# Placing keys by TensorE and giving more steps a choice of engine in a gated-attention kernel

## The chip, the core and the metric

One core of a Trainium2 chip runs the whole program. The metric is the device time of one execution in microseconds (us), the median of several. A profiled execution has its own time, and the profile's span lies inside it.

## What is computed

The input x has 2 batches of 2048 rows of 512 numbers; a context has 77 rows per batch. Four steps follow one another, each added to x with a gate:

```
x = x + tanh(g_xattn[0]) * attention0(layernorm(x), ctx, mask, Wq, bq, Wk, bk, Wv, bv, Wo, bo)  # 16 heads of 32
x = x + tanh(g_ffn[0])   * int8_matmul(layernorm(x), rhs)            # rows rounded to int8 by their absmax
x = x + tanh(g_xattn[1]) * attention1(layernorm(x), ctx, Wq, Wk, Wv, Wo, bo)  # 16 heads of 64
x = x + tanh(g_ffn[1])   * prototypes(layernorm(x), ...)  # top 2 of 32 experts of rank 16
layernorm(x) = (x - mean) / sqrt(var + 1e-5)
```

All products must be nearly f32: most operands are kept as two f16 parts (high and low), and a product is made of three f16 products.

## The kernel before, in words

The 4096 rows are 32 tiles of 128 rows; up to 11 tiles are in work at once. Each tile passes through L0, F0, L1 and M1, the four steps above. Ahead of them stands the preparation, which begins with the weights' loading and overlaps the first tiles: prepK, prepQ and prepV make keys, queries' weights and values of layer 0, prepA and prepU fold layer 1's keys and values into the weights (tiles A and U), prepR rounds rhs, prepM prepares the prototypes. prep0b and prep1b make the same tables for the second batch; they go to DRAM and come back when tile 16 begins.

**Who sets the order.** Nothing is issued where it is written. Every call is recorded by the class Clock with a cost for its engine, its port and its inputs. Where a step may go on one of several engines, `first_of` records all of them (`tt`, `cpy`, `zero` use it). After recording, `refine` places all instructions forward and backward several times, choosing for each the engine that ends it first; then `kick` shifts due times at random by seeds from the list `kicks`, and an order is kept when its planned end is earlier. What comes out is one fixed list per engine. Each engine works through its list in order, so a late instruction holds back everything behind it. All DMAs are issued by SyncE (SP), in one list too.

**The filler.** `lulls` looks for planned gaps of TensorE within the first 270 us and fills them with matmuls on a constant tile, `heat`, which write to a bank that nobody reads (L1737). There are 126 of them: 44 ahead of the first projection, 82 later. They keep TensorE busy and compute nothing.

**Keys of layer 0 (build_k).** The scores of a head are one matmul over 128 rows: queries stand as high, high, low parts of 32 rows each and 32 rows of a constant; the keys (`kst`) as high, low, high parts and rows with mask and bias. ScalarE and VectorE split the keys `kf` (128 rows are 4 heads of 32) into the f16 parts in a buffer; 12 DMAs then move 32-row pieces of them to their rows in `kst`. The bias rows come from 8 matmuls per two batches with `bsel` into 4 rows, another split, and further DMAs, in the first batch over DRAM (`kb_d`).

**Values of layer 0 (build_v).** For each f16 part a zeroed buffer is filled in four 32-row pieces by ScalarE from `vf`, for the low part also by VectorE; matmuls with slices of the identity (`ipad`) then place them.

**Layer norm (ln).** VectorE takes mean and variance, GpSimd adds EPS and scales (128x1), GpSimd raises to the power -1/2, VectorE makes the negated mean term and then the normalised row in one 128x512 step. **hl_T** makes the f16 high part with a ScalarE copy (128x512), the low part with a GpSimd subtraction, and transposes both by DMA. **probs_T** does the same to probabilities of 128x1232. **F0** rounds to int8 by adding and taking away a large constant, both on ScalarE.

A line that most instructions carry in the profile, L468, is the line of the recorder; they are told apart by their tiles.

Of the kernel before, what the change touches and what calls it, by code (L numbers as in the profile page):

```python
# [21 lines left out]
P = 128  # L22
# [83 lines left out]
class Clock:  # L106
# [272 lines left out]
    def kick(self, seed, start, last):  # L379

        rng = np.random.RandomState(seed)
        width, amp = rng.choice([40.0, 120.0, 2000.0]), rng.choice([0.5, 1.5, 4.0, 10.0])
        at = rng.rand() * max(last)
        z = rng.randn(max(self.block) + 1) * amp
        return [t + z[b] if abs(s - at) < width else t for s, t, b in zip(start, last, self.block)]
# [137 lines left out]
def first_of(choices, *a):  # L523

    alts = []
    for e, op, late in choices:
        outs, ins = e.parts(a, {})
        st = e.stages(op, outs, ins)
        alts.append((st, late, lambda f=getattr(e.e, op): f(*map(real, a))))
    c = e.clock  # L530
    best = min(range(len(alts)), key=lambda i: c.probe(alts[i][0], ins, outs) + alts[i][1] * alts[i][0][0][1])
    st, late, fn = alts.pop(best)
    alts.insert(0, (st, late, fn))
    c.add(fn, st, ins, outs, choices[best][0].name, alts)
@with_exitstack
def flamingo(ctx: ExitStack, tc: tile.TileContext, I, out):
    nc = tc.nc
    opt = dict(first=(11, 10, 3, 4, 3), carve=('uuuu', 'utt'), bufs=(11, 11, 4, 5, 4, 2), pol=(22, 0, 1.0, 0, -0.5), pr=(10, 0, 5, 5, 0, 0, 0, 0), keep=5, bias=(1, 0.6, 1, 0.5), win=-1, bonus=(0, 0, 0, -2), l1=1, res=(0, 1), ref=8, heat=270.0, lat=(0.05, 0.1, 1), whole=(6, 1, 1, 0, 0))
    opt["kicks"] = (200002, 200006, 200010, 200020, 200022, 200023, 200029, 200030, 200035, 200036, 200065, 200078, 200080, 200082, 200094, 200158, 200159, 200168, 200183, 200199, 200203, 200206, 200227, 200261, 200293, 200318, 200320, 200327, 200348, 200361, 200362, 200381, 200391, 200394, 200398, 200413, 200424, 200442, 200446, 200487, 200504, 200512, 200517, 200541, 200633, 200666, 200677, 200706, 200723, 200804, 200812, 200845, 200911, 200928, 200929, 200976, 201087, 201098, 201152, 201161, 201200, 201229, 201254, 201555, 201746, 201975, 202128, 202218, 202497, 202749, 203015, 203029, 203041, 203217, 203435, 203614, 203656, 203838, 203897, 204467, 204750, 204971, 205446, 205590, 205835, 205893, 206161, 206172, 206676, 206898, 207521, 207706, 208282, 208578, 209511, 211890, 212426, 212442, 212830, 212838, 213041, 213114, 213149, 213243, 213251, 213257, 213277, 213358, 213478, 213509, 213654, 213776, 213865, 213994, 214325, 214334, 214336, 214408, 214502, 214813, 216675, 216876, 217994, 218441, 218747, 220507, 220570, 222551, 223022, 230339, 230361)
# [12 lines left out]
    def cpy(*a):  # L552
        first_of(((V, "tensor_copy", bias_[1]), (SC, "copy", 0.0)), *a)

# [83 lines left out]
    def f16v(t):  # L638
        return t.bitcast(F16)
# [192 lines left out]
    kb_d = dr.tile([2, H, S], F16, tag="kb_d", name="kb_d")  # L832
# [11 lines left out]
    sBb = ct("sBb", [P, NB])  # L844

    def build_k(b, dst):


        t = yield from acq("E")
        hl = f16v(t)[:, : 8 * S].rearrange("p (a g s) -> p a g s", a=2, g=4)  # L850
        split(hl[:, 0], hl[:, 1], kf[:, :, b * S : (b + 1) * S], sKb[:, b : b + 1])
        m = kst[96:] if b == 0 else f16v(t)[96:, 8 * S : 8 * S + FL].rearrange("p (h s) -> p h s", s=S)
        cpy(m, mk[96:, b, :].unsqueeze(1).broadcast_to([32, H, S]))
        for i, a in enumerate((0, 1, 0)):
            for j in range(4):
                d = dst[32 * i : 32 * i + 32].rearrange("p (g j) s -> p g j s", j=4)
                SY.dma_start(out=d[:, :, j, :], in_=hl[32 * j : 32 * j + 32, a])
        yield True
        yield from until("bsel", "q")
        ps2 = mm(), mm()  # L860
        bl = f16v(t)[:4, 8 * S + FL : 16 * S + FL].rearrange("p (a g s) -> p a g s", a=2, g=4)
        for g2, ps in enumerate(ps2):
            for g in range(2):
                PE.matmul(ps[:4, g * S : (g + 1) * S], bsel[:, 2 * g2 + g, :], kf[:, 2 * g2 + g, b * S : (b + 1) * S],
                          start=True, stop=True)
            gs = slice(2 * g2, 2 * g2 + 2)
            split(bl[:, 0, gs], bl[:, 1, gs], ps[:4, : 2 * S].rearrange("p (g s) -> p g s", g=2), sBb[:4, b : b + 1])
        d = (kb_d if b == 0 else dst[96:98]).rearrange("a (g j) s -> j a g s", j=4)
        for a in range(2):
            SY.dma_start(out=d[:, a], in_=bl[:, a])  # L870
        if b == 0:
            SY.dma_start(out=dst[96:98], in_=kb_d)
        else:
            SY.dma_start(out=dst[98:], in_=m[2:])
        rel("E", t)
        yield True
# [14 lines left out]
    bsel = ct("bsel", [P, 4, 4])  # L891

    def prepB():
        zero(bsel)
        for j in range(4):
            V.tensor_copy(bsel[32 * j : 32 * j + 32, :, j], bq[32 * j : 32 * j + 32, :])
        yield True
        yield from until("rowd")
        SC.activation(tg, gv, AF.Tanh)
        V.tensor_scalar(gb0, row[:, :D], tg[:, 0:1], None, ALU.mult)  # L900
        V.tensor_scalar(cf, tg[:, 2:3], 2.0 ** -11, None, ALU.mult)
        V.tensor_scalar(mk, mk, -1.0, 1.0, ALU.mult, ALU.add)
        V.tensor_scalar(mk, mk, 0.0, -1.0, ALU.is_equal, ALU.add)
        V.tensor_reduce(anyv, mk, AX.X, ALU.max)
        V.tensor_scalar(anyv, anyv, 1.0, None, ALU.add)
        for b in range(NB):
            V.tensor_scalar(mk[:, b, :], mk[:, b, :], anyv[:, b : b + 1], BIG, ALU.mult, ALU.mult)
        sw["row"] = True
        sw["bsel"] = True
        yield True  # L910

    def prepQ():
        w = yield from wget("wq0")
        yield from norm2(1, w, wq0h.rearrange("p k n -> p (k n)"))
        absmax(17, bq)
        V.tensor_tensor(mx[:, 1:2], mx[:, 1:2], mx[:, 17:18], ALU.max)
        yield True
        sWq = pow2_of("sWq", gmax("amQ", 1, 2))
        yield from until("kf")
        V.reciprocal(c0, S_["K"])  # L920
        V.tensor_scalar(c0, c0, 2.0 ** 32, None, ALU.mult)
        V.tensor_tensor(sWq, sWq, c0, ALU.min)
        V.tensor_tensor(c0, sWq, S_["K"], ALU.mult)
        V.tensor_scalar(sBb, anyv, c0, 1.0 / (512.0 * BIG), ALU.mult, ALU.mult)
        V.reciprocal(c0, c0)
        V.tensor_scalar(c0, c0, 512.0 * 32.0 ** -0.5, None, ALU.mult)
        sw["c0"] = True
        split(wq0h, wq0l, w, sWq)
        yield True
        wrel("wq0")  # L930
        sw["q"] = True


    def build_v(b, v0):
        for hl in range(2):
# [3 lines left out]
            for j in range(4):  # L939
                r = slice(32 * j, 32 * j + 32)  # L940
                c = slice(128 + j * S, 128 + (j + 1) * S)
                src = vf[r, :, b * S : (b + 1) * S]
                SC.activation(vbd[r, :, c], src, AF.Copy, scale=S_["V"][r, :])
                if hl:
                    V.scalar_tensor_tensor(vbd[r, :, c], src, S_["V"][r, :], vbd[r, :, c],
                                           ALU.mult, ALU.subtract)
            yield True
            for half in range(2):
                ps = mm()
                for q in range(5):  # L950
                    k = half * 5 + q
                    h0, h1 = blk_heads(k)
                    o = ps[:, q * 96 : q * 96 + 96]
                    gs = sorted({h // 4 for h in range(h0, h1)})
                    for i, g in enumerate(gs):
                        w0 = 128 + 128 * k - 308 * g
                        st = 96 - 32 * (4 * g - h0)
                        PE.matmul(o, vbd[:, g, w0 : w0 + 128], ipad[:, st : st + 96],
                                  start=(i == 0), stop=(i == len(gs) - 1))
                cpy(v0[:, hl, half * 5 : half * 5 + 5, :],  # L960
                        ps[:, :480].rearrange("p (q n) -> p q n", n=96))
                yield True
            rel("E", vs)

# [22 lines left out]
    def prep0b():  # L987

        yield from build_k(1, kst1_d)
# [285 lines left out]
    def ln(c):  # L1275
# [7 lines left out]
        G.tensor_scalar(rr, mv[:, 1:2], EPS, 2.0 ** -22, ALU.add, ALU.mult)  # L1283
# [4 lines left out]
        V.scalar_tensor_tensor(xn, xt, rr, m.broadcast_to([P, D]), ALU.mult, ALU.add)  # L1288
# [3 lines left out]
    def hl_T(xn):  # L1292
        hl = yield from acq("u")
        h = f16v(hl)
        SC.copy(h[:, :D], xn)
# [10 lines left out]
    def probs_T(E, pack):  # L1306
# [3 lines left out]
        SC.copy(ph[:, :FL], E)  # L1310
# [116 lines left out]
    def F0(c):  # L1427
# [8 lines left out]
        SC.activation(xn, xn, AF.Identity, bias=magic, scale=iv)  # L1436
# [3 lines left out]
        SC.activation(h, xn, AF.Identity, bias=unmagic)  # L1440
# [344 lines left out]
```

## Time and profile before

| What | Value |
|---|---|
| Median of 3 runs | 978.26 us (977.76 to 978.44) |
| Profiled execution: time, span | 980.5 us, 978.7 us |
| Busy: PE (TensorE) | 940.9 us, 96%, 6306 instructions |
| Busy: ACT (ScalarE) | 756.6 us, 77% |
| Busy: DVE (VectorE) | 749.2 us, 77% |
| Busy: POOL (GpSimd) | 644.8 us, 66% |
| Chain that ended last, by engine | PE 60%, DVE 16%, DMA 7%, ACT 7%, POOL 5%, issue 3% |

PE is TensorE's matmuls, PEld its weight loads. A busy PE need not be PE at its peak, because matmuls are pipelined and overlap their records: a 512-column matmul has a record of 379 ns, but the next one starts about 215 ns later. An f32 matmul leaves two records. A group's row names line, engine, operation, output<-input, the shape and the count; behind the bar stand the engine's idle time just before it, and what ended that.

### The profile page before, as it was taken

How to read it: one execution, taken by the hardware profiler on the slowest of the kernel's cores; microseconds unless marked ns; L12 is line 12 of the kernel's file. 1: busy time of each engine (PE TensorE's matmuls, PEld its weight loads, DVE VectorE, ACT ScalarE, POOL GpSimd, SP SyncE). 2: the span in 40 equal slices, each digit the busy share in tenths (PEclk: the TensorE clock that was granted, in tenths of full speed). 3: DMA queues.
4: the chain of work that ended last, by engine and by line, in shares of the span. 5: the costliest groups of instructions: out<-in, count | busy, mean ns of one | idle time of the engine just before them, and what ended most of it. 6: DMA issues, size and time to landing. Idle time of an engine off the chain costs nothing.

```text
span 978.7 us, 20530 instructions
## 1 busy us (share of the span) xinstructions
PE 940.9 (96%) x6306; PEld 512.8 (52%) x6306; DVE 749.2 (77%) x2153; ACT 756.6 (77%) x2669; POOL 644.8 (66%) x808
## 2 busy tenths in 40 slices
PE   9987889999999999999999999999999999999998
PEld 6865444555555555555455544545554555445543
DVE  3898879888978876886896788679787877865574
ACT  2878979998878798676899689677985899637521
POOL 2346568988668377667676966777668667654652
PEclk9998999999999999999999999999999999999999
DMA  9589996569999989999887899988479767753354
GB/s 318 189 216 199 165 210 132 116 137 175 200 192 187 186 164 189 180 155 192 169 166 153 152 229 204 186 147 156 83 160 191 154 109 159 124 102 71 71 113 124
DMA packets 491423, 159.67 MB, mean 163 GB/s; under 512 B 472113, under 2 KB 472625, under 8 KB 491185
## 3 DMA queue, kind: packets, MB, share of 16 engines
q1 hardware_dynamic: 491313, 158.37, 81.2%
q8 instruction: 49, 0.80, 0.3%
q14 instruction: 61, 0.50, 0.2%
HBM read 32.58 MB, written 14.35 MB: 48 GB/s over the span
## 4 chain that ended last, share of the span: by engine, by line
PE 60%; DVE 16%; DMA 7%; ACT 7%; POOL 5%; issue 3%; SPq 0%; DVEq 0%; POOLq 0%; ACTq 0%
PE bank L468 58%; DVE bank L468 5%; ACT E L468 5%; DVE s_x L468 4%; DVE u L468 2%; PE bank L1737 2%; DMA u<-W 2%; DVE x L468 2%; POOL u L468 1%; DMA u<-u 1%; POOL pp L468 1%; DMA v<-u 1%; POOL s_x L468 1%; POOL E L468 1%; ACT u L468 1%
## 5 line engine op out<-in xcount | busy, mean ns | idle before, releaser
L468 ACT ACTIVATE E<-bank,s_x,c 128x77 f32<-128x77 f32 x1024 | 412.9, 432 | 44.3 <-DVE s_x L468 39.0
L468 PEld LDWEIGHTS <-u 128*128 128x128 f16 x2324 | 198.3, 97 | 191.0 <-DMA u<-W 7.5
L468 ACT ACTIVATION_READ_ACCUMULATOR E<-bank,s_x,c 128x1 f32 x1024 | 225.7, 220 | 0.0
L468 PE MATMUL bank<-A,u 128*128 128x462 f16 (+1 forms) x864 | 190.6, 336 | 5.2 <-DVE x L468 1.7
L468 POOL TENSOR_TENSOR pp<-E,pp 128x1232 f16<-128x1232 f32 (+3 forms) x128 | 172.0, 1355 | 25.2 <-ACT pp L468 18.0
L468 PEld LDWEIGHTS <-W 128*128 128x128 f16 (+1 forms) x1540 | 119.7, 98 | 111.7 <-DMA W<-u 4.1
L468 PE MATMUL bank<-U,pt 128*128 128x512 f16 (+1 forms) x646 | 175.3, 379 | 0.0
L468 DVE TENSOR_REDUCE bank<-bank 128x6 f32<-128x462 f32 (+1 forms) x192 | 112.6, 587 | 37.2 <-PE bank L468 30.7
L468 PEld LDWEIGHTS <-pt 128*128 128x128 f16 (+1 forms) x1256 | 93.7, 98 | 84.5 <-DMA pt<-pp 8.9
L468 POOL TENSOR_SCALAR s_x<-s_x 128x1 f32<-128x1 f32 (+1 forms) x160 | 32.5, 203 | 113.4 <-DVE s_x L468 103.9
L468 DVE SCALAR_TENSOR_TENSOR x<-bank,c,x 128x512 f32<-128x512 f32 x96 | 71.1, 742 | 39.8 <-PE bank L468 39.5
L468 DVE BATCH_NORM_STATS2 s_x<-x 128x6 f32<-128x512 f32 x128 | 87.8, 686 | 7.9 <-DMA x<-x_dram 6.6
L468 ACT CAST pp<-E 128x1232 f16<-128x1232 f32 x64 | 78.3, 1226 | 17.5 <-POOL E L468 17.0
L468 POOL TENSOR_TENSOR u<-u,u 128x512 f16<-128x512 f32 x61 | 70.6, 1162 | 27.6 <-ACT u L468 26.8
L468 POOL TENSOR_TENSOR E<-E,s_x 128x1232 f32<-128x1232 f32 x32 | 71.9, 2248 | 22.9 <-DVE s_x L468 19.6
L468 PE MATMUL bank<-U,W 128*128 128x512 f16 x282 | 79.2, 379 | 0.2 <-DMA W<-pp 0.2
L468 POOL TENSOR_TENSOR s_x<-s_x,mhalf 128x1 f32<-128x1 f32 x128 | 70.0, 548 | 8.5
L468 PE MATMUL bank<-AA,u 128*128 128x512 f16 x228 | 67.0, 379 | 0.0
L468 PE MATMUL bank<-BB,u 128*128 128x512 f16 x228 | 66.5, 379 | 0.1
L468 ACT CAST u<-u 128x512 f16<-128x512 f32 x61 | 38.0, 624 | 31.3 <-DVE u L468 23.5
L468 DVE SCALAR_TENSOR_TENSOR u<-x,s_x,bank 128x512 f32<-128x512 f32 x75 | 55.4, 742 | 1.2 <-POOL W L468 0.2
L468 PE MATMUL bank<-wq0h,u 128*128 128x512 f16 x168 | 49.0, 379 | 0.8 <-ACT s_x L468 0.8
(331 smaller groups left out, 1791.5 us busy)
## 6 DMA issues: line engine op xcount, KB each, us to landing
x<-x_dram SPq DMA_DIRECT2D x32, 256.0 KB, 3.1
out_dram<-x SPq DMA_DIRECT2D x32, 256.0 KB, 2.4
A_d<-pp SPq DMA_DIRECT2D x8, 308.0 KB, 5.7
U_d<-pp SPq DMA_DIRECT2D x8, 308.0 KB, 5.7
A<-A_d SPq DMA_DIRECT2D x1, 2464.0 KB, 9.6
U<-wk1T_dram SPq DMA_DIRECT2D x2, 1024.0 KB
W<-wq_dram SPq DMA_DIRECT2D x2, 1024.0 KB, 15.4
A<-wv1T_dram SPq DMA_DIRECT2D x2, 1024.0 KB
```

Of the source, the lines that this page charges most:

```text
L468: self.clock.add(lambda: f(*map(real, a), **{n: real(v) for n, v in k.items()}), self.stages(op, outs, ins, ALU.pow in a), ins, outs, self ...
L1737: prog.append((t, -1, lambda b=b: nc.tensor.matmul(b, heat[:, :P], heat, start=True, stop=True)))
```

## The change

1. **build_k** places keys by TensorE. The split parts and a bias-and-mask part are made for all 128 rows; 16 matmuls per batch with 32-column slices of the identity put each 32-row piece in its rows of a bank (308 columns each); four copies on VectorE or ScalarE move the banks to `kst`. The bias row comes from 16 small f32 matmuls per batch (32 rows by 32 columns, 77 wide) in place of 4 with `bsel`. All DMAs of build_k go, `kb_d` and `bsel` too; the second batch's table is written to DRAM by one DMA.
2. **build_v** splits the values of all 128 rows in two instructions; the four pieces per part are copied by ScalarE or GpSimd.
3. **Choice of engine**: `first_of` takes alternatives with arguments of their own. The f16 copies in hl_T and probs_T (`half`) may go on ScalarE or GpSimd; layer norm's last step on VectorE or GpSimd; both steps of F0's rounding on ScalarE or GpSimd.
4. **ln**: adding EPS and scaling moves from GpSimd to VectorE, in all 128 layer norms.
5. `kick` draws other times, widths, amounts and shares of blocks, and the list of its seeds is another. So the whole order is planned anew.

The diff, cut to its core:

```diff
+    def half(*a):
+        first_of(((SC, "copy", 0.0), (G, "tensor_copy", 0.0)), *a)
...
     def build_k(b, dst):
-        hl = f16v(t)[:, : 8 * S].rearrange("p (a g s) -> p a g s", a=2, g=4)
+        o = 4 * S
+        hl = f16v(t)[:, : 2 * o].rearrange("p (a g s) -> p a g s", a=2, g=4)
         split(hl[:, 0], hl[:, 1], kf[:, :, b * S : (b + 1) * S], sKb[:, b : b + 1])
-        for i, a in enumerate((0, 1, 0)):
-            for j in range(4):
-                d = dst[32 * i : 32 * i + 32].rearrange("p (g j) s -> p g j s", j=4)
-                SY.dma_start(out=d[:, :, j, :], in_=hl[32 * j : 32 * j + 32, a])
...
+        for g in range(4):
             for j in range(4):
+                r = slice(32 * j, 32 * j + 32)
+                PE.matmul(ps[r, g * S : (g + 1) * S], bq[r, g : g + 1].broadcast_to([32, 32]),
+                          kf[r, g, b * S : (b + 1) * S], start=True, stop=True)
...
+        SC.activation(h, pv, AF.Copy, scale=sBb[:, b : b + 1])
+        V.scalar_tensor_tensor(z, pv, sBb[:, 2 + b : 3 + b], mk[:, b, :].unsqueeze(1).broadcast_to([P, 4, S]),
+                               ALU.mult, ALU.add)
+        V.scalar_tensor_tensor(h, h, hot[:, 2:3], z, ALU.mult, ALU.add)
+        for j in range(4):
+            ps = mm()
+            one = ipad[:, 96 + 32 * j : 128 + 32 * j]
+            for i, src in enumerate((hl[:, 0], hl[:, 1], hl[:, 0], h)):
+                PE.matmul(ps[32 * i : 32 * i + 32, :o], one, src, start=True, stop=True)
+            cpy(dst.rearrange("p (g j) s -> p j g s", j=4)[:, j], ps[:, :o].rearrange("p (g s) -> p g s", g=4))
...
     def build_v(b, v0):
+        split(parts[:, 0], parts[:, 1], vf[:, :, b * S : (b + 1) * S], S_["V"])
...
-                SC.activation(vbd[r, :, c], src, AF.Copy, scale=S_["V"][r, :])
-                if hl:
-                    V.scalar_tensor_tensor(vbd[r, :, c], src, S_["V"][r, :], vbd[r, :, c],
-                                           ALU.mult, ALU.subtract)
+                first_of(((SC, "copy", 0.0), (G, "tensor_copy", 0.0)), vbd[r, :, 128 + j * S : 128 + (j + 1) * S], parts[r, hl])
...
     def prep0b():
-        yield from build_k(1, kst1_d)
+        yield from build_k(1, k1)
+        SY.dma_start(out=kst1_d, in_=k1)
...
     def ln(c):
-        G.tensor_scalar(rr, mv[:, 1:2], EPS, 2.0 ** -22, ALU.add, ALU.mult)
+        V.tensor_scalar(rr, mv[:, 1:2], EPS, 2.0 ** -22, ALU.add, ALU.mult)
         G.tensor_tensor(rr, rr, mhalf[:, :1], ALU.pow)
...
-        V.scalar_tensor_tensor(xn, xt, rr, m.broadcast_to([P, D]), ALU.mult, ALU.add)
+        first_of(((V, "scalar_tensor_tensor", 0.0, (xn, xt, rr, m.broadcast_to([P, D]), ALU.mult, ALU.add)),
+                  (G, "tensor_scalar", 0.0, (xn, xt, mv[:, 0:1], rr, ALU.subtract, ALU.mult))))
...
     def hl_T(xn):
-        SC.copy(h[:, :D], xn)
+        half(h[:, :D], xn)
...
     def probs_T(E, pack):
-        SC.copy(ph[:, :FL], E)
+        half(ph[:, :FL], E)
...
     def F0(c):
-        SC.activation(xn, xn, AF.Identity, bias=magic, scale=iv)
+        first_of(((SC, "activation", 0.0, (xn, xn, AF.Identity), dict(bias=magic, scale=iv)),
+                  (G, "tensor_scalar", 0.0, (xn, xn, iv, MAGIC, ALU.mult, ALU.add))))
...
-        SC.activation(h, xn, AF.Identity, bias=unmagic)
+        first_of(((SC, "activation", 0.0, (h, xn, AF.Identity), dict(bias=unmagic)),
+                  (G, "tensor_scalar", 0.0, (h, xn, MAGIC, None, ALU.subtract))))
```

## The prediction

> **What bounds the kernel now.** I read the page's busy times first, then the same by windows, then PE in order of time, then the chain that ended last. In the fence below, each row by windows gives the stretch, its length, the busy times of PE, PEld, DVE, ACT and POOL, PE's granted clock, the DMA share and GB/s.
>
> ```profile
> PE 940.9 (96%) x6306; PEld 512.8 (52%) x6306; DVE 749.2 (77%) x2153; ACT 756.6 (77%) x2669; POOL 644.8 (66%) x808
> ...
> 56.00:68.00 12.00, 9.18 (x62) 6.58 (x60) 11.76 (x20) 9.51 (x16) 5.12 (x8) 1.00 0.69 164
> 68.00:77.00 9.00, 7.17 (x55) 5.04 (x56) 8.69 (x29) 7.93 (x35) 4.57 (x6) 1.00 0.87 213
> 77.00:84.00 7.00, 0.58 (x14) 0.54 (x11) 6.82 (x20) 7.00 (x24) 4.47 (x4) 0.82 1.08 193
> 84.00:90.00 6.00, 6.00 (x51) 5.87 (x49) 4.80 (x13) 4.23 (x14) 2.11 (x2) 0.65 0.91 200
> ...
> 160.00:974.00 814.00, 801.85 (x5341) 421.03 (x5339) 623.55 (x1813) 634.41 (x2324) 565.36 (x701) 1.00 0.81 155
> ```
>
> From 160 us on PE is busy for 801.85 of 814 us: PE bounds there, and all other engines together can give back only the 12.15 us in which it sits idle. Before 160 us it is different. From 56 to 84 us DVE is busy for 27.3 of 28 us and ACT for 24.4 of 28, PE for 16.9. That is where PE waits for others. And what PE does there is partly nothing:
>
> ```profile
> L1737 PE MATMUL bank<-heat 128*128 128x512 f16 x126 | 33.8, 402 | 1.6 <-DVE heat L1734 1.4
> ...
> 23.61 1.29 PE bank L1737 x6
> ...
> 83.74 1.49 PE L468 MATMUL bank<-v,pt 128*128 128x64 f16 x20 [6.42 <-DVE pp L468]
> ```
>
> The 126 filler matmuls are counted as busy. The chain's row gives 1.29 us for six, 0.215 us each. They mark planned gaps: a filler stands in PE's list where the plan had nothing real to do. The last row is the longest wait of PE, 6.42 us before 83.74 us; after it the granted clock falls to 0.65 in the 6 us from 84 to 90. So there are three purses: fillers (82 behind the first projection, 17.6 us), waits of PE before 160 us (about 20 us), and 12 us later.
>
> **The change, part by part.** *The fillers.* The order of the two built programs, engine by engine, shows what was planned: 55 fillers in place of 126, 49 ahead of the first projection (before 44) and 6 later (before 82). 71 go: 71 x 0.215 = **-15.3 us** of PE's list. The five more at the start (1.1 us) are within this sum. This is a count in the program, not a time; whether the gaps go on the chip is the question of the first rival.
>
> *Real matmuls added.* The lists have 5944 real matmuls before and 6000 after: 32 new of 32 output rows by 308 columns, 32 new f32 of 32x77, and 8 f32 of 4x77 less. None of the new forms is in the trace. By columns a 308-wide f16 one takes 308/512 x 0.215 = 0.129 us; the nearest row of the small f32 ones is below, four matmuls in eight records, 0.70/4 = 0.175 us each.
>
> ```profile
> 21.83 0.70 PE L468 MATMUL bank<-kf,bsel 128*4 128x77 f32 x8
> ```
>
> So 32 x 0.129 + 32 x 0.175 - 8 x 0.175 = 4.1 + 5.6 - 1.4 = **+8.3 us**. Bounds: at 0.038 us each, the step between 77-wide f16 matmuls on kst, 64 cost 2.4 and the net is +1.0; at the full record of a 308-wide one (294 ns), with no overlap, 18.8 and +17.4. They can't cost less than nothing, because PE gets 56 more matmuls and loses no other real one. I take the middle value, which goes by columns as every wide row does.
>
> The Trainium skill (TensorE: Matmul & The Clock Gate, "Measured speedup vs the span model") reports that three matmuls in different 32-column strips of the array run 2.38 times as fast as one after another. No row here has such strips, so the trace can neither back nor deny it; by that figure the 308-wide ones would cost 1.7 in place of 4.1 us and the forecast would be about 2.4 us lower.
>
> *build_k's DMAs and its latency.* SP's list loses 29 issues net. For the first batch the 12 issues to kst hold SP for 2.54, 2.85, 1.93 and 1.90 us between 42 and 63 us, and the last lands in the chain:
>
> ```profile
> 59.41 1.28 SPq L468
> 60.74 0.43 SPq L468
> 61.22 2.00 DMA kst<-E
> ```
>
> In their place come matmuls, and four bank copies whose nearest rows are 0.415 us (ACT, 128x308 from a bank) and 0.645 us (DVE, 480 columns). Kst's first reader stood behind 198 real matmuls, now behind 184, of about the same work, so the keys are due no earlier in the list; but what feeds them no longer stands in SP's queue between transposes. The 6.42 us wait and the lost clock behind it (0.35 x 6 = 2.1 us) come from this crowded stretch, 8.5 us in all. DVE's list there doesn't get much shorter (next paragraph), so I count half as gone: **-4.3 us**. Ends: 0 and -8.5.
>
> *Loads.* In SP's list the row of masks goes from eighth to second place and wo0 from sixth to twelfth, with 6.2 MB ahead of it; at the 318 GB/s of the first slice it lands near 23 us. On ACT its norm stands ahead of the splitting of wq0 and of copies to kst. ACT reached wo0 at 25.2 us before, so some 2 us of cover hide it; without them every further microsecond delays kst by the same.
>
> *Engines.* The lists show what the choices became. ACT gives 45 casts of 128x512 (0.62 us), 16 rounding steps (about 0.78) and 14 casts of 128x1232 (1.23) to POOL: 27.9 + 12.5 + 17.2 = 57.6 us less. DVE gives 31 last steps of layer norm (0.742 us): 23.0 less, and the 8 pieces of values at 0.663, 5.3 less; it gets 128 scalings of 128x1 at its own 0.20 us, 25.6 more, and six wide splits. The values' 16 pieces on ACT (0.552) give way to 14 copies of the same shape, which about cancels. So DVE's total stays, and ACT is the one that is relieved. POOL loses the 128 scalings (0.196 each, 25.1) and gets 47 steps and 45 copies of 128x512 and 14 of 128x1232. None of these is in the trace on POOL. Bounds per 512 columns: a memset of 256 columns takes 0.312, so 0.62; a two-input step 1.157. For 1232: 1.50 and 2.52. Together 78 to 142 us; POOL comes to 698 to 762 us, 72 to 79% of the span. I take the low end, as these steps have one wide input. Then a copy costs on POOL what it costs on ACT, and no path gets longer. Where PE is bound this is worth nothing by itself; it shows in the early stretch, and I count it there with the 8.5 us and not twice. The moved scaling lengthens nothing: 0.196 us on POOL becomes 0.20 on DVE with the same crossing to the power step.
>
> A price that the low end leaves out is seen here:
>
> ```profile
> L468 DVE TENSOR_SCALAR rq<-U x4: 420/424/1378, 74.7 to 81.7; 128x512 f16<-128x512 f32 x4
> ```
>
> The same DVE step takes 0.42 us, and 1.38 us when POOL's two-input step of 81.63 us lies beside it. The skill says why (GPSIMD Engine Reference, "Key points"): GpSimd shares its SBUF interfaces with VectorE, and they contend when VectorE uses two ports or two SBUF inputs. That speaks against moving work to POOL. But most wide DVE steps here read a bank, and the last step of layer norm keeps 0.714 to 0.749 us over all its 75 rows, so I add nothing for it.
>
> *Sum.* Against the profiled execution: span 978.7 - 15.3 + 8.3 - 4.3 = 967.4 us. Its own time is 980.5, the median of the runs 978.26, so in the median's terms 978.26 - 11.3 = **967.0 us**.
>
> **Rivals.** (1) *The early stretch opens wholly.* The 8.5 us go, and the relieved ACT also halves the 12.15 us of PE's late idle time: 978.3 - 15.3 + 8.3 - 8.5 - 6.1 = 956.7, with the new matmuls at their low end 949. For it: ACT is busy for 77.6 of 80 us from 160 to 240. Against it: PE is busy for 79.6 of the same 80.
>
> (2) *The change doesn't do what it says: gaps come back as waits.* The old plan also had fewer gaps than the chip showed: about 20 us of waits beside 17.6 us of fillers. A list without gaps has no slack, and if half of the 15.3 us returns as waits and the 6.42 us wait stays, 978.3 - 7.0 + 7.7 = 979.0: no change. For it: DVE's load stays as it was. Against it: the waits before were there on top of the fillers, not in place of them.
>
> (3) *POOL becomes the bound: slower.* At the upper prices each moved 512-column step is 0.54 us longer than on ACT and each 1232 one 1.0, 64 us in all. POOL's list is in order, and behind a late copy stands the subtraction for the low part, its transpose, and then PE. It decides where POOL has no idle time: from 160 to 240 us it is busy for 70.8 of 80, and the second eighth of its list, by the upper prices, grows by 9 us, to the full 80. If a quarter of the 64 us comes through, 967.0 + 16 = 983. Against it: the plan puts such steps on POOL only where it was free by its own costs.
>
> **How the numbers follow.** Forecast 0.55, rival 1 0.20, rival 2 0.12, rival 3 0.13. The range of 8 in 10 runs from 954 to 979: it leaves out rival 3 and the lower end of rival 1, and takes in the bounds of the new matmuls (-7.3, +9.1) about the forecast. A difference under 0.2%, 976.3 to 980.2, can't be told from no change. Rival 2 is spread about it: 0.07 same, 0.03 faster, 0.02 slower. Together faster 0.55 + 0.20 + 0.03 = 0.78, same 0.07, slower 0.02 + 0.13 = 0.15.
>
> **What would show it.** Right: PE's busy time near 940.9 - 15.3 + 8.3 = 934 us, no single wait of PE over 3 us from 56 to 90 us, the clock at 1.00 there, ACT near 699 us, POOL near 698. Wrong: PE idle before 160 us above 28 us (rival 2), POOL's copies of 128x512 near 1.1 us and ACT's or SP's waits for POOL grown in the middle (rival 3), or wo0's norm on ACT waiting past 25 us.

## The result, and the profile after

The changed kernel takes 984.38 us (median of 4 runs, 983.57 to 985.54), the kernel before 978.01 on the same chip: a ratio of 1.0053 (95% interval 1.0035 to 1.0071). Measured again beside the last experiments it has 982.11 against 977.18, 1.0052 (1.0037 to 1.0068). It is slower by half a per cent; 967.0 was forecast. The profiled execution took 985.54 us, its span is 983.6.

The busy times of the changed kernel's page, then its stretches (length, busy PE, PEld, DVE, ACT, POOL, PE's granted clock, DMA share, GB/s):

```profile
PE 938.8 (95%) x6315; PEld 512.9 (52%) x6315; DVE 747.5 (76%) x2250; ACT 706.9 (72%) x2596; POOL 743.5 (76%) x786
```

```profile
56.00:68.00 12.00, 5.44 (x43) 4.10 (x43) 11.61 (x37) 10.83 (x32) 4.65 (x6) 0.80 1.03 309
68.00:77.00 9.00, 3.98 (x13) 3.32 (x14) 8.78 (x19) 8.72 (x39) 8.05 (x7) 0.50 0.79 194
77.00:84.00 7.00, 7.00 (x50) 4.62 (x50) 5.49 (x19) 2.65 (x9) 0.00 (x0) 0.77 0.06 14
84.00:90.00 6.00, 6.00 (x61) 5.88 (x59) 5.85 (x14) 5.94 (x16) 5.11 (x4) 1.00 0.96 165
160.00:974.00 814.00, 796.56 (x5352) 419.11 (x5351) 620.69 (x1895) 595.70 (x2261) 648.28 (x681) 1.00 0.80 154
```

ACT is relieved nearly as forecast (706.9 us for 699). POOL has 743.5 us, 45 more than the low prices gave. The fillers went as counted, but PE's granted clock is 0.50 to 0.80 from 56 to 84 us, where it was 1.00 to 0.82: PE waits there and then runs at half speed. From 160 us on PE sits idle for 17.4 us instead of 12.15. The one wait of 6.42 us is gone; by PE in order of time, waits of one to three microseconds stand ahead of its place, all for DVE or POOL (the bracket is the idle time and what ended it):

```profile
66.09 1.07 PE L470 MATMUL bank<-kst,u 128*128 128x77 f16 x10 [2.07 <-DVE s_x L470]
68.52 0.47 PE L470 MATMUL bank<-eye,mx 128*128 128x128 f32 x1 [1.35 <-POOL mx L470]
70.67 2.94 PE L470 MATMUL bank<-E,W 128*128 128x154 f32 x10 [1.68 <-DVE cb L470]
```

PE's idle time before 160 us is 23.5 us against 21.7, although 15.3 us of fillers are gone from there; what fell is the clock, 0.85 from 56 to 160 us against 0.97. Which kernel is ahead is better seen by the work done. For this estimate each matmul that both kernels have is priced at the mean step from its start to the next one's, of its form, in the three traces after 160 us (0.216 us for 512 columns; 898.7 us in all). The table gives the time, in us, at which a given amount was done; the last column is a kernel of the experiments below, with POOL's fast forms:

| PE work done, us | before | changed | changed, POOL's fast forms |
|---|---|---|---|
| 100 | 159.0 | 154.8 | 151.6 |
| 150 | 210.1 | 214.5 | 211.1 |
| 400 | 465.0 | 471.3 | 465.0 |
| 600 | 672.2 | 675.0 | 666.1 |
| 860 | 935.9 | 940.8 | 927.6 |

The changed kernel is 4.2 us ahead at about 155 us and 4.4 behind at 214. So there was a gain, and something takes it back where PE had almost never waited. It is not POOL's forms: the last column needs 59.5 us for the same work, the changed kernel 59.7, the kernel before 51.1. PE's waits are 3.8 us of the difference and the second batch's new matmuls 2.4 net; the rest was not separated. What the last column gains on the changed kernel in these profiled executions, 3.2 us by 155 us and 13.2 in the end, comes ahead of this stretch and behind it.

POOL's groups in the changed kernel hold a row that the prediction did not allow for (busy us, mean ns of one):

```profile
L533 POOL TENSOR_SCALAR u<-x,s_x 128x512 f32<-128x512 f32 x22 | 45.8, 2082 | 1.0 <-DMA u<-u 0.3
...
L533 POOL CAST u<-u 128x512 f16<-128x512 f32 x18 | 11.1, 621 | 3.9 <-DVE u L533 2.3 <-PE bank L470 0.6 <-DVE s_x L470 0.5
...
L533 POOL TENSOR_SCALAR u<-u 128x512 f16<-128x512 f32 x2 | 3.0, 1501 | 0.1
```

The copies cost 0.62 us, the low end, as forecast. Layer norm's last step costs 2.08 us, above the upper bound of 1.157; 31 of them ran on POOL (22 into u, the rest into W and k). The rounding back from int8, 8 of them, costs 1.50 each.

### The profile page after: what moved, and what is told of

Its sections match the earlier page's. It is cut to its first block, busy times and chain, and to the rows that moved or that the text cites. A ratio compares the mean times of both kernels' runs of the same rounds, so it can differ in the third digit from the quotient of the medians.

```text
span 983.6 us, 20508 instructions
## 1 busy us (share of the span) xinstructions
PE 938.8 (95%) x6315; PEld 512.9 (52%) x6315; DVE 747.5 (76%) x2250; ACT 706.9 (72%) x2596; POOL 743.5 (76%) x786
## 5 line engine op out<-in xcount | busy, mean ns | idle before, releaser
L470 PEld LDWEIGHTS <-u 128*128 128x128 f16 x2144 | 180.8, 98 | 181.4 <-issue 14.7
L470 POOL TENSOR_TENSOR pp<-E,pp 128x32 f16<-128x32 f32 (+3 forms) x128 | 172.0, 1355 | 20.3 <-ACT pp L533 18.9
L470 PE MATMUL bank<-A,u 128*128 128x462 f16 (+1 forms) x648 | 147.9, 339 | 3.2 <-DMA u<-u 2.7
L470 PEld LDWEIGHTS <-pt 128*128 128x128 f16 (+2 forms) x1287 | 92.6, 98 | 79.8 <-DMA pt<-pp 6.1
L470 PE MATMUL bank<-U,W 128*128 128x512 f16 (+1 forms) x301 | 81.8, 379 | 1.5 <-DMA W<-pp 1.5
L533 ACT CAST pp<-E 128x1232 f16<-128x1232 f32 x50 | 61.1, 1222 | 23.7 <-POOL E L470 20.5
L470 POOL TENSOR_TENSOR u<-u,u 128x512 f16<-128x512 f32 x54 | 62.4, 1156 | 15.3 <-ACT u L533 14.3
L470 PE MATMUL bank<-A,W 128*128 128x462 f16 (+1 forms) x324 | 72.7, 336 | 0.0
L470 DVE TENSOR_SCALAR s_x<-s_x 128x1 f32<-128x1 f32 x320 | 53.7, 172 | 12.1 <-POOL s_x L470 4.6
L470 DVE TENSOR_SCALAR bank<-s_x 128x1 f32<-128x1 f32 x128 | 27.9, 218 | 24.8 <-POOL s_x L470 18.9
L533 POOL TENSOR_SCALAR u<-x,s_x 128x512 f32<-128x512 f32 x22 | 45.8, 2082 | 1.0 <-DMA u<-u 0.3
```

The source lines that it names most:

```text
L470: self.clock.add(lambda: f(*map(real, a), **{n: real(v) for n, v in k.items()}), self.stages(op, outs, ins, ALU.pow in a), ins, outs, self ...
L533: f(*map(real, q), **{n: real(v) for n, v in k.items()})))
```

## The experiments

Unless it is said otherwise, an experiment keeps the order of all instructions of the kernel that it is made from, so that only the named thing differs.

**The fillers by themselves.** The kernel before, without the 82 fillers behind the first projection:

```diff
-heat=270.0
+heat=2.0
```

> The kernel before with the same order, but without the 82 filler matmuls behind the first projection; the 44 ahead of it stay. The prediction priced a removed filler at 0.215 us of PE's list: 82 x 0.215 = 17.6 us less, 960 us. Theory 'fillers hold the clock': PE's list was waiting at these places anyway, so the fillers' time comes back as idle time of PE, and the granted clock falls in the early stretch besides: 978 to 988 us, granted clock below 0.99 over the span. A time near 960 would leave the prediction's first step standing.

975.39 us against 977.23, ratio 0.9984 (0.9974 to 0.9994). 82 fillers are worth 1.8 us, not 17.6. PE waited at these places in any case, and without fillers it waits visibly and slows: from 56 to 160 us its clock is 0.87 instead of 0.97 (the kernel before, then this run), and the long wait is still there (6.56 us, up to 81.83).

```profile
56.00:160.00 104.00, 83.87 (x614) 50.22 (x613) 90.87 (x231) 90.34 (x297) 63.62 (x77) 0.97 0.91 182
56.00:160.00 104.00, 79.97 (x565) 50.18 (x566) 89.97 (x235) 92.15 (x302) 65.55 (x79) 0.87 0.85 179
```

Of the 17.6 us, 8.3 come back as idle time of PE before 160 us (30.0 us, where it was 21.7). By difference most of the rest, some 7 us, went into matmuls at the lower clock.

**Fillers put into the changed kernel.** 69 of them, at 13 of its early waits:

```diff
+FILL = {189: 3, 200: 2, 214: 3, 218: 7, 222: 2, 228: 8, 238: 5, 239: 6, 244: 11, 381: 5, 451: 3, 457: 7, 470: 6}
+        for n, k in FILL.items():   # ahead of the n-th real matmul
+            for j in range(k):
+                prog.append((s0, -1, lambda b=b: nc.tensor.matmul(b, heat[:, :P], heat, start=True, stop=True)))
```

> The changed kernel in its own order, with 69 fillers added at thirteen places of PE's list where its trace shows waits of 0.5 to 2.8 us before 120 us, each sized a little below the wait. Theory 'fillers hold the clock': the granted clock in the stretch from 56 to 120 us goes from 0.5 to 0.8 back to 1.00, and the time falls by 4 to 9 us, to 975 to 981. Theory 'POOL's price' alone, or fillers as pure cost: the time stays at 983 to 986 or grows by up to 15 us (69 x 0.215).

981.53 us, ratio 1.0049 (1.0035 to 1.0064). The profiled clock rises from 0.984 to 0.993, PE's idle time before 160 us falls from 23.5 to 13.2 us, and the time stays: what the fillers give in clock and idle time they take in time of their own. This does not price the half clock by itself. It isn't what separates the kernels, though: the kernel with POOL's fast forms below has a clock of 0.87 from 56 to 160 us, the changed kernel 0.85, and they are 9.6 us apart.

**Layer norm's last step back on VectorE**, all 31:

```diff
+        for i in back:
+            sel[i] = next(k for k, a in enumerate(ck.ops[i][0]) if a[0][0][0] == "DVE")
```

> The changed kernel in its own planned order, with one thing undone: the 31 last steps of layer norm that the plan gave to POOL (2.08 us each in its trace) go back to VectorE (0.744 us), at the same places. Theory 'POOL's price': late rows of layer norm are what PE waits for, so the time falls from 984.4 to about 972 (968 to 977), and POOL's busy time falls by 64 us to about 680. Theory 'clock and early stretch': the steps lie beside other work; the time stays within 981 to 986.

982.6 us, ratio 1.0055 (1.0039 to 1.0071): no gain, though POOL's busy time falls to 679 us. I took this for proof that POOL's price of this step decides nothing. That was wrong, as the next runs showed.

**What makes the step dear.** The kernel before with five forms of one 128x512 f32 step on POOL, three times over, at its end (one run, no ratio):

```diff
+        nc.gpsimd.tensor_scalar(xb, xa, p0, p1, ALU.subtract, ALU.mult)
+        nc.gpsimd.tensor_scalar(xb, xa, p0, p1, ALU.mult, ALU.add)
+        nc.gpsimd.tensor_scalar(xb, xa, p0, 0.5, ALU.subtract, ALU.mult)
+        nc.gpsimd.tensor_scalar(xb, xa, p0, None, ALU.mult)
+        nc.gpsimd.tensor_scalar(xb, xa, 2.0, 0.5, ALU.mult, ALU.add)
```

> The kernel before with 15 GpSimd steps of 128x512 in f32 added behind everything, three of each of five forms on an idle tile, to measure the price by itself: two scalars from a tile (subtract then multiply, as in the changed layer norm; and multiply then add), one from a tile with a constant, one from a tile alone, and two constants. Theory 'two scalars from a tile are the dear ones': the first two 2.08 us, the other three about 0.69. Theory 'the place of the output is dear' (layer norm writes another tile, the int8 rounding writes in place): all five near 2.08. The span grows by 15 to 30 us, which says nothing else.

POOL in order of time, the five forms in the diff's order (start, duration):

```profile
962.23 2.08 POOL L1747 TENSOR_SCALAR x<-x,mhalf,phalf 128x512 f32<-128x512 f32 x1
964.42 0.76 POOL L1748 TENSOR_SCALAR x<-x,mhalf,phalf 128x512 f32<-128x512 f32 x1
965.28 2.00 POOL L1749 TENSOR_SCALAR x<-x,mhalf 128x512 f32<-128x512 f32 x1
967.38 1.57 POOL L1750 TENSOR_SCALAR x<-x,mhalf 128x512 f32<-128x512 f32 x1
969.04 0.62 POOL L1751 TENSOR_SCALAR x<-x 128x512 f32<-128x512 f32 x1
```

Both explanations on record fall. It is neither the two scalars from tiles nor the place of the output, but the operations: the same operands cost 0.76 us as multiply and add and 2.08 as subtract and multiply, and one multiply alone costs twice the pair. The Trainium skill (GPSIMD Engine Reference, "Elementwise — side-by-side cycle accounting") gives 769 ns for 512 elements in its best loop; the 0.76 agrees with multiply and add, and the run adds that pairs which begin with a subtraction take 2.00 to 2.08 us.

**POOL's forms in the changed kernel.** Layer norm's step as x*r + (-mean*r), which is the same value up to rounding, the rounding back as times 1 plus a constant. The edit, in short:

```diff
-    G.tensor_scalar(xn, xt, mv[:, 0:1], rr, ALU.subtract, ALU.mult)
+    G.tensor_scalar(xn, xt, rr, ms, ALU.mult, ALU.add)      # ms = -mean*rr, in SBUF
-    G.tensor_scalar(h, xn, MAGIC, None, ALU.subtract)
+    G.tensor_scalar(h, xn, 1.0, -MAGIC, ALU.mult, ALU.add)
```

> The changed kernel in its own order; layer norm's last step on POOL is written as multiply and add (x*r - mean*r, with -mean*r put in SBUF) instead of subtract and multiply, and POOL's rounding back of int8 as times 1 plus a constant instead of subtract. By the run of forms the step should take 0.76 us instead of 2.08, 31 times. Theory P (POOL's price for the subtract form): POOL's busy time falls by 35 to 45 us and the time by 2 us or more, ratio under 1.0035. Theory D (the earlier run with these steps on VectorE, ratio 1.0055, had already shown that this price decides nothing): POOL's busy time falls just as much and the ratio stays at 1.0045 to 1.006.

> The changed kernel in its own order with only POOL's two steps as multiply and add, once more, since its first measurement had a wide interval (0.9991 to 1.0034): 0.9985 to 1.002 if that was right; under 0.997 if it is this alone that turns the result, with the loads adding little.

> The changed kernel in its own order with POOL's two steps as multiply and add, a third time, because its first two measurements, on two chips, gave 1.0013 (0.9991 to 1.0034) and 0.9956 (0.9939 to 0.9973). If the second was right: 0.994 to 0.9975. If the first: 0.999 to 1.0035.

> As the run before, but only layer norm's last step is multiply and add; POOL's four roundings back keep the subtract with one constant (1.50 us each). If the 31 steps at 2.08 us are the cause: within 0.0015 of the run before. If the four roundings matter: 0.002 or more above it.

> The changed kernel in its own order with the 31 last steps of layer norm on VectorE, a second time, beside the same steps on POOL in the fast form. Theory P (POOL's time at these steps is the cause, and VectorE, which gets 20 us of work for the 44 that POOL loses, is as full): 1.004 to 1.007, as at first, while POOL's fast form is below 0.998 on the same chip. If the first value was only a spread between chips: within 0.002 of POOL's fast form.

Both forms together, measured three times: 1.0013 (0.9991 to 1.0034) on a chip where the kernel before itself ranged from 978 to 985 us; then 0.9956 (0.9939 to 0.9973) and 0.9954 (0.9938 to 0.9970; 972.14 against 977.31 us). The profiled spans of the three are 972.9, 972.2 and 970.4, but the first one's profiled execution (974.75 us) was the fastest of its twelve (median 981.37). I go by the last two, which agree on two chips; on the first chip the changed kernel itself was not measured, and why the value was higher there stays open. Layer norm's step alone (eight roundings left at 1.50 us, not four, as the expectation has it): 0.9986 (0.9976 to 0.9995). On the same chip the step on VectorE: 1.0050 (1.0037 to 1.0063), as at first.

So with POOL's two forms mended the loss becomes a gain: from 1.0052 to 0.9954, 9.6 us, for 47.5 us less of POOL's time. Layer norm's step has 40 of these and 6.5 us of the time, the roundings 7 and 3. This kernel, the table's last column, does all the work and beats both. POOL's row in it, to be held against the one above:

```profile
L1755 POOL TENSOR_SCALAR u<-x,s_x 128x512 f32<-128x512 f32 x22 | 16.9, 767 | 8.9 <-DVE s_x L1753 5.0 <-issue 2.3 <-PE bank L470 0.9
```

Before these steps POOL now sits idle for 8.9 us, where it was 1.0: at these steps POOL was the late one, not what feeds it. By stretches, first the kernel before, then the changed kernel, then that with POOL's fast forms, then that with the step on VectorE:

```profile
160.00:400.00 240.00, 237.17 (x1622) 131.78 (x1620) 191.93 (x533) 209.60 (x750) 177.27 (x216) 1.00 0.92 172
400.00:880.00 480.00, 470.91 (x3179) 243.41 (x3177) 376.48 (x1084) 382.11 (x1413) 338.75 (x419) 1.00 0.83 158
```

```profile
160.00:400.00 240.00, 230.93 (x1611) 128.51 (x1610) 188.59 (x541) 193.79 (x703) 192.52 (x203) 1.00 0.95 174
400.00:880.00 480.00, 471.62 (x3200) 244.70 (x3199) 375.14 (x1139) 364.75 (x1429) 398.15 (x410) 1.00 0.80 156
```

```profile
160.00:400.00 240.00, 233.68 (x1637) 130.59 (x1635) 190.17 (x551) 195.97 (x712) 185.86 (x209) 1.00 0.94 177
400.00:880.00 480.00, 477.21 (x3249) 248.86 (x3247) 376.80 (x1157) 369.66 (x1463) 369.89 (x412) 1.00 0.79 153
```

```profile
400.00:880.00 480.00, 471.83 (x3203) 245.00 (x3202) 385.25 (x1158) 363.72 (x1430) 354.89 (x385) 1.00 0.79 154
```

From 400 to 880 us PE idles for 8.4 us in the changed kernel, 2.8 with the fast forms, 8.2 with the step on VectorE, where POOL has the least work of all three and VectorE 10 us more than in the changed kernel. (The kernel before idles for 9.1 us there; it was ahead from 160 to 400 us, with 2.8 us against 9.1 and 6.3.) Apart from PE no engine is full in any of them. I read it so: the lists are in order, and a late step holds what stands behind it, whichever engine it is late on. With the step on VectorE, that engine's two largest waits, both for PE, shrink from 46.5 to 30.0 us in this stretch, so it had less slack. That fits, but no run took VectorE's lateness away alone.

**The two loads of 1 MB.** BB<-Bt and AA<-At are issued at 116.8 and 125.9 us in the changed kernel (119.6 and 127.5 before), beside transposes, two of which PE waits for: 2.45 us up to 136.19 and 0.59 up to 137.14. Only the loads' first quarter is moved here, so part of layer 1's mixture is computed from other numbers; the same in the kernel before. The edit, in short:

```diff
-nc.sync.dma_start(out=t, in_=v)
+nc.sync.dma_start(out=t[:, 0:1], in_=v[:, 0:1])
```

> The changed kernel in its own order, but of the two 1 MB loads BB<-Bt and AA<-At (issued at 116.8 and 125.9 us) only the first quarter is moved; the rest of the two tables keeps older contents, so that part of layer 1's mixture is computed from other numbers. In the changed kernel six transposing DMAs beside these loads land 7.0 to 8.8 us after their issue, against 3.3 us elsewhere, and PE then waits 2.8 and 0.95 us at 136 us. Theory L (these loads hold up the transposes, and that is a part of the loss): the transposes issued between 110 and 130 us land within 4 us, the wait at 136 us is under 1 us, and the time falls by 2.5 to 4 us, to a ratio of 1.0015 to 1.003 against the kernel before (the changed kernel has 1.0053). Theory O (the new order of the work as a whole, no single cost): the wait moves to the next thing, and the ratio stays at 1.0045 or above.

> The kernel before with the same two loads cut to their first quarter, so that part of layer 1's mixture is computed from other numbers. There the loads are issued at 119.6 and 127.5 us, beside fewer transposes, which land in 3.7 to 4.3 us. Theory L (the collision is new in the changed kernel): little to gain here, under 1.2 us, ratio 0.9988 to 1.0. If the loads cost both kernels the same, this one falls by 2.5 us or more (ratio 0.9975 or less), and they explain no difference.

Ratios 1.0035 (1.0019 to 1.0051) and 0.9993 (0.9977 to 1.0009). By the trace it is four transposes, not six, that land 7.7 to 8.8 us after their issue, and PE's waits are the two above, not 2.8 and 0.95. DMA issues from 110 to 132 us (median us to landing), changed kernel, then with the loads cut:

```profile
U<-pp SPq DMA_TRANSPOSE x3, 7.7
u<-u SPq DMA_TRANSPOSE x2, 5.7
```

```profile
U<-pp SPq DMA_TRANSPOSE x4, 3.9
u<-u SPq DMA_TRANSPOSE x2, 3.2
```

The transposes land sooner, though the two behind the first load's quarter still take 5.4 and 4.7 us; of the time only 1.7 us follow, and the interval still overlaps that of the whole kernel. These runs were on the chip where POOL's forms had come out at 1.0013.

**The three together, and in pairs.** Loads cut, POOL's forms and the 69 fillers; then without the loads, then without the fillers:

> The changed kernel in its own order with three things together: the two loads cut to a quarter (values of layer 1's mixture are not the reference's), layer norm's last step on POOL as multiply and add, and the 69 fillers at the early waits of the run before. If each of the three removes a wait of its own, their gains add: some 3 + 2 + 1 us, a ratio near 0.999. If a wait that one removes is only taken over by the next (theory O), the sum is no better than the best of the three alone, a ratio of 1.002 or above.

> The changed kernel in its own order with POOL's two steps as multiply and add and the 69 fillers, both loads whole. Adding up the runs alone (1.0013 and -0.0004): 1.001. If the fillers are worth more once POOL is no longer late (the three together gave 0.9956, 0.0035 less than the sum of the three alone): 0.997 to 0.999.

> The changed kernel in its own order with POOL's two steps as multiply and add and the two loads cut to a quarter (values of layer 1's mixture are not the reference's), no fillers. Adding up the runs alone (1.0013 and -0.0018): 0.9995. If these two are the pair that gives more together than alone: 0.996 to 0.998, and the fillers add nothing.

The last two ran beside the changed kernel itself:

> The changed kernel itself, unchanged, beside the next three on one chip: by its first measurement a ratio of 1.0053 (1.0035 to 1.0071).

In this order: 0.9956 (0.9939 to 0.9973); 0.9988 (0.9976 to 0.9999); 0.9917 (0.9898 to 0.9935). Against POOL's forms alone (0.9955) the cut loads give 0.004 more. The fillers give nothing. Whether they cost anything stays open: 0.9988 with them stands beside 0.9955 without, but in the next runs both have 0.9962; 0.9956 and 0.9917 come from two chips, the first from the one just named.

**The loads whole, but in four pieces each** between the transposes (all the work is done), with POOL's forms and fillers, without fillers, and alone:

> The changed kernel with POOL's two steps as multiply and add, the 69 fillers, and the two 1 MB loads whole, but issued in four pieces each between the transposing DMAs, so that a transpose never waits behind more than 256 KB. If it is the bulk ahead of a transpose that costs: transposes issued between 110 and 130 us land within 4.5 us and the ratio comes within 0.002 of the kernel with the loads cut (0.9956), below 0.9985, faster than both kernels. If it is the amount moved in that stretch, or the last piece is now late for ScalarE: no better than the kernel with the loads whole (0.999 to 1.001).

> The changed kernel in its own order, nothing left out: POOL's two steps as multiply and add, the two 1 MB loads in four pieces each between the transposes, no added fillers. With fillers this gave 0.9962 and with the loads cut and no fillers 0.9917. If the fillers cost time once the rest is mended (0.9956 against 0.9917): 0.990 to 0.994, the fastest whole kernel. If the four pieces cost what they save: 0.996 to 0.999.

> The changed kernel in its own order with only the two loads in four pieces each between the transposes. Theory L: as good as the loads cut (1.0035), between 1.0025 and 1.004. Theory O: no gain without POOL's form, 1.0045 or above.

0.9962 (0.9948 to 0.9976), 0.9962 (0.9951 to 0.9974), 1.0045 (1.0028 to 1.0061). Transposes are quicker in the pieces' kernel:

```profile
U<-pp SPq DMA_TRANSPOSE x3, 4.5
u<-u SPq DMA_TRANSPOSE x2, 3.5
```

The time does not follow: 0.9962 beside 0.9955 for the loads in one piece, and 1.0045 beside 1.0052. So the theory that the transposes' wait behind the loads costs the changed kernel its gain falls. Why the cut version is faster was not separated; it moves 1.5 MB less, and that is no saving to be had.

## Why the prediction was wrong, step by step

Two steps carry the miss: the fillers' 15.3 us, of which some 1.6 came, and the low price of POOL's steps, which cost 9.6 us where nothing was counted.

**Fillers, -15.3 us: wrong.** This step made most of the forecast. It took planned gaps for time of PE that a better plan gives back. The kernel before without 82 of them is only 1.8 us faster, which makes 1.6 for 71. A filler stands where PE would wait; taking it out saves only what it delays, and what it saved came back as idle time and as a lower clock. Rival 2 named the first half of this ("gaps come back as waits") and was given 0.12; for the second the prediction had no term.

**Real matmuls, +8.3: too high, by some 3.** By the steps from one start to the next, the new matmuls are cheap where they stand side by side (the changed kernel, PE in order of time):

```profile
23.33 0.46 PE L470 MATMUL bank<-kf,cols 32*32 32x77 f32 x12
23.71 0.53 PE L470 MATMUL bank<-ctxT,U 128*128 128x154 f32 x2
...
32.11 0.32 PE L470 MATMUL bank<-E,ipad 128*32 128x308 f16 x4
32.35 1.05 PE L470 MATMUL bank<-ctxT,U 128*128 128x154 f32 x6
33.34 0.30 PE L470 MATMUL bank<-E,ipad 128*32 128x308 f16 x1
33.58 0.79 PE L470 MATMUL bank<-ctxT,U 128*128 128x154 f32 x4
```

Twelve records of the small ones take 0.38 us from start to start, and four of the 308-wide ones 0.24 instead of 4 x 0.129. But one alone takes 0.24 too, and the plan has set nine of the 32 alone and four in twos. All 64 records together take 2.7 us, where 5.6 was counted, and the 32 wide ones 3.7, where 4.1 was; less the 1.4 removed this is +5.0 us. The column strips of the Trainium skill (TensorE: Matmul & The Clock Gate, "Measured speedup vs the span model") were weighed here and the row by columns was taken. Four side by side are 2.15 times as fast as by columns, near the page's 2.38 for three; over all 32, as they stand in the list, the price by columns was the nearer one.

**build_k, -4.3: not measured by itself.** The wait of 6.42 us is gone, but PE's idle time before 160 us has not fallen. The sum of these three steps, -1.6 + 5.0 - 4.3, is -0.9; the kernel with POOL's fast forms measures -5.0 (972.45 against 977.48, means of its two later medians). The remaining 4.1 us, and the share of each, were not separated. In the profiled executions that kernel is level with the one before at 465 us; its gain comes later, where PE idles 6.3 us less from 400 to 880 us (3.5 more from 160 to 400). That is the size that rival 1 gave to the relieved ACT (6.1 us); whether ACT made it was not tested.

**Loads: right.** wo0 lands at 24.63 us and ACT reads it at 30.72; nothing waits for it.

**Engines, nothing added for POOL: the step that turned the sign.** "I take the low end, as these steps have one wide input" holds for the copies (0.621 and 1.208 us) and fails for 39 steps: 31 at 2.08 and 8 at 1.50. An operation with two tile scalars had no row on POOL in the trace of before, and its bound was taken from instructions of another kind. The bound was too low, and the choice inside it too: 47.5 us of POOL and 9.6 us of time. The kernel's own planner made the same mistake; it prices any such step at 0.26 + 0.0009 x 512 = 0.72 us (the last lines of Engine.stages), so it put the steps where POOL seemed free.

**Rival 3 (POOL late, 983 us) had the right engine, at 0.13.** Its share was near: it let a quarter of POOL's excess through, and 9.6 of 47.5 us came through. Its place was not: it asked for a stretch where POOL has no idle time, and POOL is busy for 80% from 160 to 400 us. Its test, copies near 1.1 us, missed too: the copies were quick and the arithmetic slow. That its 983 met the measured 984 is luck: its base of 967.0 was some 5 us too low and its 16 us some 6 too high.

**Contention, nothing added: not separated.** The row that stood for it has become longer at a bad place. DVE and POOL of the changed kernel in order of time:

```profile
72.30 2.74 DVE L470 TENSOR_SCALAR U<-U 128x512 f32<-128x512 f32 x1
```

```profile
72.18 2.58 POOL L470 TENSOR_TENSOR pp<-E,pp 128x1232 f16<-128x1232 f32 x1
```

The DVE step ends 0.28 us after POOL's; its sisters take 0.42 us. The kernel before has a copy of 4x127 that takes 2.30 us at 137.84, and no run took such a case away alone. With the steps that became fast it can have had little to do: DVE's busy time fell only from 747.5 to 743.9 us with them.

## What to carry to other kernels

Before a step is given to another engine, measure it there in just the form in which it will run: on POOL the same operands took 0.76 or 2.08 us by the choice of operations. A gap or a filler in the bound engine's list is not time to be won; take the fillers out of the old kernel first and see what comes back. And where putting a step back changes nothing, make it cheap where it is before calling its price harmless: the first test took the work from POOL, gave it to VectorE and gained nothing, and yet its price on POOL was 6.5 us of the time.

## What the runs showed of the hardware that was not expected

- POOL, 128x512 f32, TENSOR_SCALAR: subtract then multiply 2.08 us, subtract with a tile's scalar then multiply by a constant 2.00, multiply alone 1.57, multiply then add 0.76 with two tile scalars and 0.62 with constants; a copy to f16 0.62. A second operation can make the step cheaper.
- Keeping PE's clock up with fillers gained nothing here: 69 of them raised the mean clock from 0.984 to 0.993, took 10.3 us from PE's idle time before 160 us and did not move the time (1.0049 against 1.0052).
- The two transposing DMAs issued next after each 1 MB load landed after 7.7 to 8.8 us; those ahead of the loads, from 110 us on, after 2.4 to 3.3. Behind a quarter of a load it was 3.3 to 5.4.
- Four f16 matmuls of 32 output rows and 308 columns, one behind the other in PE's list, took 0.24 us in all from start to start; one alone took 0.24 as well.
